# Layer 0's context quantisation: keys and values between the two turnings of the block maxima, and the fourth context's maxima one step sooner

## The chip, the cores and the metric

The kernel runs on one core of one Trainium2 chip. The metric is the device time of one execution in microseconds (us); lower is better. Engines are named as in the profile: PE is TensorE's matmul (PEld its weight loads), DVE VectorE, ACT ScalarE, POOL GpSimd, SP SyncE, which issues most DMAs.

## What is computed

A two-layer block on `x` (4 batches of 512 rows of 512) with a context `ctx_2048` (4 x 512 x 512). Cut to what matters:

```python
x = x + tanh(g_xattn[0]) * L0_xattn(layernorm(x), ctx_2048)
x = x + tanh(g_ffn[0])   * L0_ffn(layernorm(x), w1, w2)
x = x + tanh(g_xattn[1]) * L1_xattn(layernorm(x), ctx_2048, ctx_2048, ...)
x = x + tanh(g_ffn[1])   * L1_ffn(layernorm(x), ...)        # experts and a shared part
...
def L0_xattn(x, weight):                  # weight is the context
    xq = quant_dequant_act_1x128(x)       # FP8 rounding, one scale per row and 128 columns
    wq = quant_dequant_weight_128x128(weight)   # one scale per 128x128 block: its largest magnitude
    return einsum('emk,enk->emn', xq, wq)
...
K = (key @ Wk);  V = (value @ Wv)         # in L1_xattn, from the context as it was given
```

Layer 0 needs the context rounded block by block; layer 1's keys K and values V need it unrounded. `L0_ffn` has two products with weights rounded to -1, 0 and 1, rows rounded to 8 bits ahead of each, and two gelus between.

## The kernel before

**Row tiles and steps.** The 2048 rows are 16 tiles of 128 rows; tile t belongs to batch and context b = t // 4. `x_sb` holds all rows in SBUF. Layer 0 is a software pipeline written out by hand: `step(s, between)` runs for s = -7 to 15 and puts pieces of several tiles next to one another. For step s: the LayerNorm, the row maxima and the FP8 rounding of tile s+7 (`cross_rows`), the hidden scales of tile s-1 (`hidden_scales`, with the 128x2048 reduce `ham`), the first FFN product and two gelus of tile s (`hidden`), the cross product of tile s+6 (`cross_product`), then whatever is given as `between`, the second FFN product of tile s-2 (`down`), and the 8-bit rounding of rows for later tiles. From the written order a scheduler makes the final order of each engine's queue; ScalarE's gelus, squares and 8-bit roundings are pinned to the written order.

**A cross product** (`cross_product`): four turnings of the rounded rows `va` into PSUM (`tpa`, L754), a copy to SBUF on ScalarE (`vTa`, L758), four products with the rounded context (`oa`, L761; two passes each in float32), and the update of `x_sb` on VectorE (L768).

**A context** (`cross_context(b)`, L663 to L723) is a generator; each `yield` ends a piece and `go(ctx, n)` runs n pieces. The pieces before the change:
1. the block maxima along the rows of the transposed context (`cam`, L671; one 128x2048 reduce for b > 0), the first turning (`tpm`, L675), the largest of each block (`cpeak`, L677), spread over 128 columns (`cwide`, L679), the second turning (L680), and the scales `csafe` and `cup` (L682 to L686);
2. the keys: four matmuls of 512 columns (`k_ps`, L690) and a ScalarE copy (L697);
3. the values: 16 matmuls of 128 columns (`v_ps`, L702) and a ScalarE copy (L709);
4. to 7. for each quarter `dc`: the context times `cup` in place (L715, VectorE), four VectorE operations of FP8 rounding (`fp8_round`, L136 to L141), and four ScalarE multiplications by `csafe` (L722).

Keys and values read the context, and L715 overwrites it, so L715 waits for the last key and value product. Layer 0's cross product for tile 4b needs context b complete.

**Buffers.** `tpm`, `k_ps`, `v_ps`, `tpa`, `ob` and `tot_ps` share a PSUM pool of two buffers (`acc`); `oa` and `h_ps` share another of three (`big`). Contexts have three SBUF buffers. The transfer of context 3 (`load_batch(3)`) is written after step -3.

**Where pieces are placed.** Context 0 runs whole ahead of the steps. Contexts 1 and 2 are cut over steps -7 to -4 and -2 to 0, context 3 over steps 2 to 4:

```python
step(-7, [lambda: go(ctx1, 3)])
step(-5, [lambda: go(ctx1, 1)] + ...)
step(-4, [lambda: go(ctx1, 3), ...])
step(-2, [lambda: go(ctx2, 2)] + ...)
step(-1, [lambda: go(ctx2, 2)] + ...)
step(0, [lambda: go(ctx2, 3), ...])
step(1)
step(2, [lambda: go(ctx3, 3)])
step(3, [lambda: go(ctx3, 2)])
step(4, [lambda: go(ctx3, 2), ...])
```

**Reciprocal square roots** are powers on GpSimd: VectorE writes the variance (`ve_a`, `ve_b`) or the sum of squares (`nc_h`, `nc_x`), GpSimd raises it (`rstd_a`, `rstd_b`, `nc_*`), and VectorE goes on with the result (`va`, `vb` at L130; `ham` at L893). `layer_norm_stats` (L116 to L127) makes `ve_a` and `rstd_a` for the four tiles of a batch.

Of the kernel before, what the change touches and what calls it, by code (L numbers as in the profile page):

```python
# [20 lines left out]
P = 128  # L21
B, S, D = 4, 512, 512
NT = B * S // P
TB = S // P
DC = D // P
# [23 lines left out]
def flamingo_kernel(  # L49
# [22 lines left out]
    nc = tc.nc  # L72
# [9 lines left out]
    def acc(name):  # L82
        return ps_acc.tile([P, 512], F32, tag="acc", name=name)
# [26 lines left out]
    kT = kv[:, : B * S].rearrange("p (b s) -> p b s", b=B)  # L110
    v_sb = kv[:, B * S : 2 * B * S].rearrange("p (t n) -> p t n", n=NG * DH)
# [22 lines left out]
    def fp8_round(y, e):  # L134

        nc.vector.tensor_scalar(  # L136
            e.bitcast(I32), y.bitcast(I32), 0x7F800000, None, ALU.bitwise_and
        )
        nc.vector.tensor_scalar(e, e, 2.0**-6, 1.5 * 2.0**20, ALU.max, ALU.mult)
        nc.vector.tensor_tensor(y, y, e, ALU.add)  # L140
        nc.vector.tensor_tensor(y, y, e, ALU.subtract)  # L141
# [417 lines left out]
    with ExitStack() as l0:  # L559
# [9 lines left out]
        with ExitStack() as ph:  # L569
# [14 lines left out]
            def load_rows(b):  # L584
                for ts in [slice(t, t + 1) for t in range(TB)] if b == 0 else [slice(b * TB, b * TB + TB)]:
                    nc.sync.dma_start(out=x_sb[:, ts, :], in_=x_t[:, ts, :])
# [3 lines left out]
            wk_sb = wkv.tile([P, DC, NG * DH], F32, name="wk_sb")  # L590
            wv_sb = wkv.tile([P, DC, NG * DH], F32, name="wv_sb")
# [71 lines left out]
            def cross_context(b):  # L663


                c = state["ctx", b]
                cb = c.rearrange("p c (n q) -> p (c n) q", q=P)

                am = small.tile([P, 16], F32, tag="cam", name=f"cam_{b}", bufs=2)
                for ns in [slice(4 * dc, 4 * dc + 4) for dc in range(DC)] if b == 0 else [slice(16)]:  # L670
                    nc.vector.tensor_reduce(  # L671
                        am[:, ns], cb[:, ns, :], AX.X, ALU.max, apply_absolute_value=True
                    )
                tp = acc(f"tpm_{b}")
                nc.tensor.transpose(tp[:16, :P], am, ident)  # L675
                peak = small.tile([16, 1], F32, tag="cpeak", name=f"cpeak_{b}", bufs=2)
                nc.vector.tensor_reduce(peak, tp[:16, :P], AX.X, ALU.max)  # L677
                wide = small.tile([16, P], F32, tag="cwide", name=f"cwide_{b}", bufs=2)
                nc.vector.tensor_copy(wide, peak.to_broadcast([16, P]))  # L679
                nc.tensor.transpose(tp[:, P : P + 16], wide, ident[:16, :16])  # L680
                safe = small.tile([P, 16], F32, tag="csafe", name=f"csafe_{b}", bufs=2)
                nc.vector.tensor_scalar_max(safe, tp[:, P : P + 16], 1e-6)  # L682
                up = small.tile([P, 16], F32, tag="cup", name=f"cup_{b}", bufs=2)
                nc.vector.reciprocal(up, safe)
                nc.vector.tensor_scalar_mul(up, up, FP8_MAX)
                nc.vector.tensor_scalar_mul(safe, safe, 1.0 / FP8_MAX)  # L686
                yield
                k_ps = acc(f"k_ps_{b}")
                for dc in range(DC):
                    nc.tensor.matmul(  # L690
                        k_ps,
                        lhsT=wk_sb[:, dc, :],
                        rhs=c[:, dc, :],
                        start=dc == 0,
                        stop=dc == DC - 1,
                    )
                nc.scalar.copy(kT[:, b, :], k_ps)  # L697
                yield
                v_ps = acc(f"v_ps_{b}")
                for kc in range(TB):  # L700
                    for dc in range(DC):
                        nc.tensor.matmul(  # L702
                            v_ps[:, kc * P : (kc + 1) * P],
                            lhsT=c[:, dc, kc * P : (kc + 1) * P],
                            rhs=wv_sb[:, dc, :],
                            start=dc == 0,
                            stop=dc == DC - 1,
                        )
                nc.scalar.copy(  # L709
                    v_sb[:, b * TB : (b + 1) * TB, :], v_ps.rearrange("p (c n) -> p c n", c=TB)  # L710
                )
                yield
                for dc in range(DC):
                    ns = slice(dc * 4, dc * 4 + 4)
                    nc.vector.tensor_tensor(  # L715
                        cb[:, ns, :], cb[:, ns, :], up[:, ns].unsqueeze(2).to_broadcast([P, 4, P]),
                        ALU.mult,
                    )
                    e = apool.tile([P, 512], F32, tag="e", name=f"ce_{b}_{dc}")
                    fp8_round(c[:, dc, :], e)  # L720
                    for n in range(dc * 4, dc * 4 + 4):
                        nc.scalar.mul(cb[:, n, :], cb[:, n, :], safe[:, n : n + 1])  # L722
                    yield  # L723
# [200 lines left out]
            def at(t, *what):  # L924
                if 0 <= t < NT:
                    for f in what:
                        f(t)

            def go(pieces, n=1):
                for _ in range(n):  # L930
                    next(pieces, None)

            def step(s, between=()):

                rows = iter(())
                if s + 7 < NT:
                    rows = cross_rows(s + 7)
                at(s - 1, hidden_scales)
                go(rows)
                at(s, hidden)  # L940
                at(s + 6, cross_product)
                go(rows)
                for f in between:
                    f()
                at(s - 2, down)
                at(s - 1, hidden_quant)
                if s % TB == 0:
                    at(s + 4, row_stats)
                    at(s + 5, row_stats)
                elif s % TB == 1:  # L950
                    at(s + 5, row_stats)
                    at(s + 6, row_stats)
                    at(s + 3, row_norm)
                    at(s + 4, row_norm)
                elif s % TB == 2:
                    at(s + 4, row_norm)
                    at(s + 5, row_norm)
                at(s + 2, row_quant)
                at(s + 1, row_ready)

            with ExitStack() as first:
                stg = first.enter_context(tc.tile_pool(name="stg", bufs=4))
                ws = (w1T, w2T)
                wd = (w1q, w2q)
                load_batch(1)
                load_rows(1)
                load_weight(stg, 0, ws[0])
                load_batch(2)
                for b in range(2, B):
                    load_rows(b)  # L970
                go(cross_context(0), 7)
                cross_stats(0)

                def w(f, k, *cs):
                    return [lambda c=c: f(k, c, wd[k]) for c in cs]

                ctx1, ctx2 = cross_context(1), cross_context(2)
                step(-7, [lambda: go(ctx1, 3)])
                step(-6, w(weight_sum, 0, 0, 1))
                step(-5, [lambda: go(ctx1, 1)] + w(weight_sum, 0, 2, 3))  # L980
                weight_mean(0)
                scales_left(0)
                step(-4, [lambda: go(ctx1, 3), lambda: cross_stats(1)] + w(weight_round, 0, 0, 1))
                load_weight(stg, 1, ws[1])
                step(-3, w(weight_round, 0, 2, 3) + w(weight_sum, 1, 0))
                load_batch(3)
                step(-2, [lambda: go(ctx2, 2)] + w(weight_sum, 1, 1, 2, 3))
                weight_mean(1)
                scales_left(1)
                step(-1, [lambda: go(ctx2, 2)] + w(weight_round, 1, 0, 1, 2, 3))  # L990
            hpool = ph.enter_context(tc.tile_pool(name="hpool", bufs=2))
            state["hpool"] = hpool
            step(0, [lambda: go(ctx2, 3), lambda: cross_stats(2)])
            ctx3 = cross_context(3)
            step(1)
            step(2, [lambda: go(ctx3, 3)])
            step(3, [lambda: go(ctx3, 2)])
            step(4, [lambda: go(ctx3, 2), lambda: cross_stats(3)])
# [327 lines left out]
    for n in range(2):  # L1326
        m, f = rt(f"m{n}", 1), rt(f"f{n}", 1)
# [17 lines left out]
    for k in range(NT):  # L1345
        nc.tensor.matmul(
            pos[:, k * E :],
            lhsT=before if k == 0 else ones_h,
            rhs=flat[:, : (NT - k) * E],
            start=k == 0,  # L1350
            stop=k == NT - 1,
        )
    for t in range(NT):
        nc.tensor.matmul(
            pos_ps[:, 1, :E],
            lhsT=ones_h,
            rhs=taken[:, t, :],
            start=t == 0,
            stop=t == NT - 1,
# [38 lines left out]
    go = []  # L1398
    for n in range(2):
        w = rt(f"w{n}")  # L1400
# [235 lines left out]
```

## Time and profile before

| | us |
|---|---|
| median of three runs | 1257.39 (1257.39 to 1257.48) |
| the profiled execution | 1256.45 |
| its span (first to last instruction) | 1254.8 |
| outside the span | 1.65 |
| mean granted TensorE clock | 0.977 of full |
| layer 0's steps with context work | about 30 to 173 of the span |

How to read the views. Times count from the start of the span. A row of the busy-time table is one stretch: its borders, its length, then for PE, PEld, DVE, ACT and POOL the busy time with the number of instructions, the granted TensorE clock (1.00 is full), the mean busy share of the DMA engines and GB/s. A row of a waits list is the engine, what waited, what released it, and then the total time, how many times, and the longest. A timeline row is start, duration, engine, line, operation, output<-inputs, shapes and how many alike in a row; in brackets stands the idle time of the engine just ahead and what ended it. A float32 matmul of 128x512 appears as two passes, so four of them are x8.

The clock row of the page, in 40 equal slices of 31.4 us (9 is 90% or more of full), shows that the granted clock is mostly full:

```profile
PEclk9887999899999999999999999999999999999998
```

And the row for VectorE in the same slices; layer 0 is the first five or six:

```profile
DVE  7999999787457666656654511331221111111110
```

### The profile page before, as it was taken

The numbers are of one execution on the slowest core, as the hardware profiler recorded it, in microseconds if no ns is written. First come the engines' busy times: TensorE is split into PE (matmuls) and PEld (weight loads), VectorE is DVE, ScalarE is ACT, GpSimd is POOL, SyncE is SP. The second block draws the span as 40 slices with busy tenths as digits, with TensorE's granted clock in tenths as the row PEclk, the third lists the DMA queues.
The fourth block names the chain that finished last, engine by engine and source line by source line (L and its number), as shares of the span: only waits on it lengthen the run. The fifth ranks groups of instructions, "written<-read, shape, count | busy, mean of one in ns | idle before, by whom it ended". The sixth has DMA issues, their size and how long they took to land. (4 is left out here: it accounts for less than half of the span.)

```text
span 1254.8 us, 14322 instructions
## 1 busy us (share of the span) xinstructions
PE 1163.9 (93%) x5262; PEld 531.2 (42%) x5262; DVE 606.4 (48%) x1157; ACT 510.8 (41%) x710; POOL 412.7 (33%) x409
## 2 busy tenths in 40 slices
PE   5776988899899999999999999999999999999996
PEld 2432443343333333333333444444345555555553
DVE  7999999787457666656654511331221111111110
ACT  4889798595355554544454211100001112121211
POOL 1010010111467877767787301055001111111111
PEclk9887999899999999999999999999999999999998
DMA  9411222445011211211003000056316786888782
GB/s 345 152 66 25 43 43 54 92 84 127 5 65 35 68 36 35 69 35 60 2 1 143 9 1 1 0 201 212 85 66 187 229 270 195 261 259 252 207 261 35
DMA packets 88753, 135.32 MB, mean 108 GB/s; under 512 B 52837, under 2 KB 54121, under 8 KB 84841
## 3 DMA queue, kind: packets, MB, share of 16 engines
q1 hardware_dynamic: 80936, 116.52, 29.3%
q0 software_dynamic: 7744, 17.86, 6.5%
q8 instruction: 42, 0.69, 0.2%
q14 instruction: 31, 0.25, 0.1%
HBM read 113.84 MB, written 32.32 MB: 116 GB/s over the span
## 5 line engine op out<-in xcount | busy, mean ns | idle before, releaser
L428 ACT ACTIVATE ex<-s,mbias,mk 128x1024 f32<-128x1024 f32 x128 | 147.3, 1201 | 140.6 <-PE s L239 140.6
L319 DVE TENSOR_REDUCE nmax<-s 128x2 f32<-128x1024 f32 x128 | 150.3, 1215 | 98.8 <-PE s L239 88.0
L1475 PE MATMUL gue<-w,xT 128*128 128x352 f32 x576 | 176.3, 459 | 0.0
L1516 POOL DMA_INDIRECT out_dram<-ye,row_i x36 | 55.5, 1542 | 317.7 <-ACT ye L1515 219.5
L389 POOL TENSOR_TENSOR part<-part,ex 128x1024 f32<-128x1024 f32 x62 | 144.7, 2353 | 16.3 <-PE sm L239 11.4
L1219 PE MATMUL gu<-xnT_d,w 128*128 128x512 f32 x320 | 140.4, 593 | 0.7 <-ACT xnT_d L1173 0.7
L1475 PEld LDWEIGHTS gue<-w,xT 128*128 128x128 f32 x576 | 109.1, 190 | 70.4 <-issue 16.9
L1498 DVE COPY hT<-tph_e 128x256 f32<-128x256 f32 x36 | 15.3, 425 | 248.6 <-PE tph_e L1495 248.6
L1506 PE MATMUL oe<-w,hT 128*128 128x512 f32 (+1 forms) x216 | 102.3, 609 | 3.2 <-DVE hT L1498 0.5
L1219 PEld LDWEIGHTS gu<-xnT_d,w 128*128 128x128 f32 x320 | 59.9, 190 | 73.9 <-issue 72.1
L1207 ACT ACTIVATE sg<-gu,sgb 128x512 f32<-128x512 f32 x20 | 13.7, 687 | 176.8 <-PE gu L1219 176.8
L761 PE MATMUL oa<-ctx,vTa 128*128 128x512 f32 x128 | 65.9, 662 | 19.1 <-ACT vTa L758 19.1
L389 POOL TENSOR_TENSOR part<-ex,ex 128x1024 f32<-128x1024 f32 x32 | 75.8, 2391 | 23.0 <-ACT ex L428 23.0
L1484 ACT ACTIVATE sge<-gue 128x352 f32<-128x352 f32 x35 | 16.3, 466 | 147.3 <-PE gue L1475 147.3
L239 PE MATMUL s<-row_tables 10*128 10x512 bf16 (+1 forms) x512 | 67.7, 384 | 9.2 <-DVE nmax L319 5.7
L239 PE MATMUL s<-k,qT 32*128 32x512 f32 x512 | 72.4, 605 | 0.4 <-ACT qT L287 0.4
L239 PE MATMUL s<-qT,k 32*128 32x512 f32 x512 | 71.6, 598 | 0.0
L912 PE MATMUL ob<-w2q,hqT 128*128 128x512 bf16 x256 | 62.2, 396 | 9.4 <-DVE hqT L838 9.4
L239 PE MATMUL av<-ex,kv 128*32 128x512 f32 x512 | 69.2, 605 | 0.4 <-ACT ex L428 0.4
L1208 DVE SCALAR_TENSOR_TENSOR hd<-gu,sub,sg 128x512 f32<-128x512 f32 x20 | 15.0, 750 | 111.5 <-ACT sg L1207 111.5
L239 PE MATMUL q_ps<-xnT,wq_sb 128*128 128x512 f32 (+1 forms) x156 | 68.6, 552 | 0.0
L239 PE MATMUL oc<-wo,attnT 128*128 128x512 f32 (+1 forms) x164 | 66.2, 525 | 0.0
(262 smaller groups left out, 1649.7 us busy)
## 6 DMA issues: line engine op xcount, KB each, us to landing
w<-in_e_w_dram SPq DMA_DIRECT2D x36, 1408.0 KB
w<-in_e_w_dram SPq DMA_DIRECT2D x36, 768.0 KB
slots<-row_tables SPq DMA_DIRECT2D x13, 771.0 KB
xr<-slots SPq DMA_DIRECT2D x36, 256.0 KB
stage<-in_w1T_dram SPq DMA_DIRECT2D x4, 1024.0 KB
stage<-in_w2T_dram SPq DMA_DIRECT2D x4, 1024.0 KB
k<-kv SPq DMA_DIRECT2D x64, 64.0 KB
out_dram<-x_sb SPq DMA_DIRECT2D x16, 256.0 KB
```

Source lines behind the costliest of these rows:

```text
L239: tc.keep_in_program_order(nc.tensor.matmul(*args, **how))
L319: largest = nc.vector.tensor_reduce(nmax[:, i, 2 * j : 2 * j + 2], sc[j], AX.X, ALU.max, negate=True)
L389: nc.gpsimd.tensor_tensor(part[:, hs, :], old[:, hs, :], ex[:, hs, :], ALU.add)
L428: nc.scalar.activation(ex[:, 2 * j : 2 * j + 2, :], sc[j], AF.Exp, bias=mbias[:, b, kc : kc + 1], scale=mk[:, b, kc : kc + 1],)
L761: nc.tensor.matmul(o_ps[:, 0, :], lhsT=vT[:, dc, :], rhs=cq[:, dc, :], start=dc == 0, stop=dc == DC - 1,)
L912: nc.tensor.matmul(o_ps, lhsT=hqT[:, c, :], rhs=w2q[:, c * D : (c + 1) * D], start=c == 0, stop=c == IC - 1,)
L1219: nc.tensor.matmul(gu[:, m, :], lhsT=w[:, dc, c * P : (c + 1) * P], rhs=xnT[:, dc, b * S : (b + 1) * S], start=dc == 0, stop=dc == DC - 1,)
L1475: nc.tensor.matmul(gu[:, m, :I], lhsT=xT[:, dc, :], rhs=wt[:, dc, :], start=dc == 0, stop=dc == DC - 1,)
L1484: nc.scalar.activation(sg, gu[:, 0, :I], AF.Silu)
L1498: nc.vector.tensor_copy(hT[:, :2, :], tp[:, : 2 * P].rearrange("p (c q) -> p c q", q=P))
L1506: nc.tensor.matmul(o_ps[:, 0, :], lhsT=hT[:ni, c, :], rhs=dw[:ni, c, :], start=c == 0, stop=c == len(ICH) - 1,)
L1516: added = nc.gpsimd.indirect_dma_start(out=out, out_offset=bass.IndirectOffsetOnAxis(ap=row_i[:, j, 0:1].bitcast(I32), axis=0), in_=y, in_ ...
```

## The change

Keys and values become an inner generator `keys_values`. For contexts 1 to 3 it now runs after `cwide` and ahead of the second turning, with one more `yield` before it; the second turning, `csafe` and `cup` follow after the values. Context 0 keeps its order. The placement follows the new count of pieces: four instead of three of context 1 in step -7, three instead of two of context 2 in step -1; and context 3's first piece (maxima, first turning, `cpeak`, `cwide`) is given to step 1, its next three to step 2.

```diff
@@ cross_context
+                def keys_values():
+                    k_ps = acc(f"k_ps_{b}")
...
+                    nc.scalar.copy(kT[:, b, :], k_ps)
+                    yield
+                    v_ps = acc(f"v_ps_{b}")
...
+                    yield
...
                 nc.vector.tensor_copy(wide, peak.to_broadcast([16, P]))
+                if b > 0:
+                    yield
+                    yield from keys_values()
                 nc.tensor.transpose(tp[:, P : P + 16], wide, ident[:16, :16])
                 safe = small.tile([P, 16], F32, tag="csafe", name=f"csafe_{b}", bufs=2)
                 nc.vector.tensor_scalar_max(safe, tp[:, P : P + 16], 1e-6)
...
                 nc.vector.tensor_scalar_mul(safe, safe, 1.0 / FP8_MAX)
                 yield
-                k_ps = acc(f"k_ps_{b}")
...
-                yield
-                v_ps = acc(f"v_ps_{b}")
...
-                yield
+                if b == 0:
+                    yield from keys_values()
                 for dc in range(DC):
...
-                step(-7, [lambda: go(ctx1, 3)])
+                step(-7, [lambda: go(ctx1, 4)])
...
-                step(-1, [lambda: go(ctx2, 2)] + w(weight_round, 1, 0, 1, 2, 3))
+                step(-1, [lambda: go(ctx2, 3)] + w(weight_round, 1, 0, 1, 2, 3))
...
-            step(1)
+            step(1, [lambda: go(ctx3)])
             step(2, [lambda: go(ctx3, 3)])
```

The matmuls and copies inside `keys_values` are those that stood there before, unchanged.

More of the change, by code (lines that the diff above doesn't have):

```diff
@@ L667, in cross_context @@
                 cb = c.rearrange("p c (n q) -> p (c n) q", q=P)
+                def keys_values():
+                    k_ps = acc(f"k_ps_{b}")
+                    for dc in range(DC):
+                        nc.tensor.matmul(
+                            k_ps,
+                            lhsT=wk_sb[:, dc, :],
+                            rhs=c[:, dc, :],
+                            start=dc == 0,
+                            stop=dc == DC - 1,
+                        )
+                    nc.scalar.copy(kT[:, b, :], k_ps)
+                    yield
+                    v_ps = acc(f"v_ps_{b}")
+                    for kc in range(TB):
+                        for dc in range(DC):
+                            nc.tensor.matmul(
+                                v_ps[:, kc * P : (kc + 1) * P],
+                                lhsT=c[:, dc, kc * P : (kc + 1) * P],
+                                rhs=wv_sb[:, dc, :],
+                                start=dc == 0,
+                                stop=dc == DC - 1,
+                            )
+                    nc.scalar.copy(
+                        v_sb[:, b * TB : (b + 1) * TB, :], v_ps.rearrange("p (c n) -> p c n", c=TB)
+                    )
+                    yield
                 am = small.tile([P, 16], F32, tag="cam", name=f"cam_{b}", bufs=2)
@@ L687, in cross_context @@
                 yield
-                k_ps = acc(f"k_ps_{b}")
[L689 to L697, printed above, removed]
-                yield
-                v_ps = acc(f"v_ps_{b}")
[L700 to L711, printed above, removed]
-                yield
+                if b == 0:
+                    yield from keys_values()
                 for dc in range(DC):
```

## Prediction, written before the changed kernel ran

> **What bounds the kernel now.** I read the page first, then busy time by stage, then the waits of TensorE and VectorE in the stage that the edit touches, then the timelines around the fourth context.
>
> ```profile
> PE 1163.9 (93%) x5262; PEld 531.2 (42%) x5262; DVE 606.4 (48%) x1157; ACT 510.8 (41%) x710; POOL 412.7 (33%) x409
> ```
>
> Over the whole span TensorE looks like the bound. That is an average. All moved instructions lie in layer 0, and in the built instruction order of the changed kernel every queue is back in the old order at the reduce `ham_5` (L888, 172.98 us on VectorE). So the stage is 29.8 to 173 us, here with the two after it:
>
> ```profile
> core 0: us, PE busy (x) PEld busy (x) DVE busy (x) ACT busy (x) POOL busy (x), PEclk, DMA share, GB/s
> 29.80:173.00 143.20, 110.30 (x404) 56.86 (x405) 136.83 (x379) 123.96 (x222) 11.99 (x12) 0.87 0.26 72
> 173.00:213.00 40.00, 32.12 (x129) 14.39 (x128) 37.38 (x106) 33.55 (x49) 3.87 (x5) 1.00 0.26 50
> 320.00:790.00 470.00, 459.67 (x2740) 170.77 (x2735) 247.51 (x267) 199.42 (x224) 285.98 (x272) 1.00 0.11 38
> ```
>
> VectorE is busy 136.83 of 143.20 us (96%), TensorE 110.30 (77%). The roles turn only later (459.67 of 470 for TensorE). VectorE leads this stage and has 6.4 us of idle time in it. The waits say whose:
>
> ```profile
> PE oa L761 <- ACT vTa L758: 15.8, 8, 7.0
> PE tpm L680 <- DVE cwide L679: 7.7, 2, 5.5
> PE k_ps L690 <- DVE csafe L682: 1.1, 1, 1.1
> ```
> ```profile
> DVE ham L893 <- POOL nc_h L788: 2.1, 4, 0.7
> DVE vb L130 <- POOL rstd_b L804: 1.8, 2, 0.9
> DVE x_sb L768 <- PE oa L761: 1.7, 3, 0.8
> ```
>
> The first list (us, times, longest) has what the edit aims at: TensorE stands at the second turning for 7.7 us. The second shows that little of it reaches VectorE, which waits for a TensorE result only 1.7 us in all. The large wait, in TensorE's queue:
>
> ```profile
> 117.16 0.33 PE L754 MATMUL tpa<-ident,va 128*128 128x128 f32 x1
> 123.00 0.28 PE L680 MATMUL tpm<-ident,cwide 16*128 16x16 f32 x1 [5.51 <-DVE cwide L679]
> 124.35 2.08 PE L690 MATMUL k_ps<-ctx,wk_sb 128*128 128x512 f32 x2 [1.07 <-DVE csafe L682]
> 126.22 4.51 PE L761 MATMUL oa<-ctx,vTa 128*128 128x512 f32 x8
> 133.14 3.73 PE L702 MATMUL v_ps<-wv_sb,ctx 128*128 128x128 f32 x32
> ```
>
> **The change part by part.** The instruction set is the same on every engine: no work is added or removed, and VectorE's 136.83 us stay. cross_context issues no DMA, SP's queue is unchanged, and POOL's only swaps one hidden-scale power with the power for `rstd_a`. Only VectorE's idle time can change, so I laid its new order out with the durations of before and took the difference of each wait.
>
> *Context 1* (three more pieces at step -7): TensorE does all 16 value products before the second turning instead of 5, turning, 11. With `v_ps_1` unsplit, `oa_0` and `oa_1` come about 0.7 us sooner, and two VectorE waits of 0.32 and 0.09 go: -0.41.
>
> *Context 2*: keys go ahead of the turning, whose first wait (7.7 - 5.5 = 2.2 us on TensorE) is filled. Values are split 6 and 10 around `oa_5`, not 8 and 8. The scaling L715 rewrites `ctx` and must wait for the last value product; VectorE now comes there earlier, and gives back +0.36. The scheduler also moves `ve_a_8` (85.35 us before) to directly ahead of `va_8`: 0.74 us of work lie between, where the same power round trip shows 1.31 to 1.73 us elsewhere in the trace (start to start). I take 1.4: +0.65 (bounds +0.57 and +0.99). Queued behind it are the LayerNorm rows of tile 8, then ACT's `va_8` scalings.
>
> *Context 3* (maxima at step 1, keys and values at step 2). The block reduce `cam_3` (2.28 us at 108.71) goes 2.6 us earlier. It then stands ahead of the x-updates L768 of `oa_6` and `oa_7`, whose waits were 0.60 and 0.76; about 0.1 of the first is left: -1.26. On TensorE the first turning goes behind `oa_7`, the second into `tpa_8`; the waits of 5.51 and 1.07 go. All four key products (3.6 us) run at about 117.7 to 121.3, in that gap. Then TensorE has nothing: `oa_8` waits for `vTa_8`, which on ACT stands behind `va_9`'s scalings (4 in 1.28 us) and the first gelu of `h_2` (2.09), and those scalings wait for `xup_9`, which VectorE now makes at 121.3, not 112.3. 121.3 + 1.28 + 2.09 + 0.5 = 125.1: a new wait of 3.8 us in place of 6.6.
>
> Here a rule bears on the sum. The rows first:
>
> ```profile
> 53.00:56.40 3.40, 1.12 (x3) 0.65 (x4) 3.40 (x9) 3.40 (x7) 0.75 (x1) 1.00 0.62 196
> 56.40:59.80 3.40, 3.40 (x6) 1.32 (x5) 3.40 (x10) 3.40 (x6) 0.64 (x1) 0.50 0.94 308
> ```
>
> A 4.00-us wait ended at 55.27 in a stretch with 1.12 us of TensorE work, yet the next 3.4 us were granted half the clock, and the eight `oa` passes took 5.40 us, not the 3.70 of a full-rate row. The Trainium skill ("TensorE: Matmul & The Clock Gate", section "What's actually happening") says that the clock halves after at least one idle window of about 3.4 us and returns after one busy window. By that rule, with the windows' phase left open, a gap of 3.8 us holds a whole idle window rarely ((3.8 - 3.4)/3.4, 12%), `oa_8` runs at full rate, and `v_ps_3` ends at 125.1 + 3.7 + 3.5 = 132.3, before VectorE needs `ctx`: no stall. By the row the clock halves until about 128.0 (the stretches lie on a 3.4-us grid, at 121.2, 124.6, 128.0): 2.9 us do 1.45 us of work, the other 2.25 end at 130.25, and values at 133.8. I take the row, as it is a measurement of such a gap.
>
> VectorE comes to `ctx_3` x `cup` (L715) at 132.8. Before it came at 136.69 and found the values just done:
>
> ```profile
> 136.37 0.41 DVE L139 TENSOR_SCALAR xe<-xe 128x512 f32<-128x512 f32 x1
> 136.69 0.68 DVE L715 TENSOR_TENSOR ctx<-ctx,cup 128x512 f32<-128x512 f32 x1
> ```
>
> Now it waits 133.8 - 132.8 = +1.0 (bounds 0 by the rule, 4.2 below). Behind the waiting instruction stand `xup_11`, the statistics of the fourth context, the `ob_0` update and `ham_2`; ACT's `va_11` scalings and `hq_2` wait for those, but ACT has slack (123.96 of 143.2 busy). Small ones: the first `vb_4` waits 1.08, not 0.91 (+0.17); `ham_0` +0.1, `oa_8` +0.1, `ham_3` +0.2; several waits under 0.1 go, -0.25. `ob_0` is 2.8 us earlier on TensorE; its reader on VectorE comes later anyway, so that is worth nothing.
>
> Sum: -0.41 + 0.36 + 0.65 - 1.26 + 1.0 + 0.17 + 0.1 + 0.1 + 0.2 - 0.25 = +0.66 us at 173 us. From there the order is identical and VectorE still leads (37.38 of 40), so the shift is carried to the end. The profiled execution took 1256.45 us (span 1254.8 and 1.65 outside it), so 1257.1; the median of the runs is 0.94 above that execution: 1257.39 + 0.66, about 1258.0 us.
>
> **The rivals.** 0.2% (2.5 us) is about what a measurement of this kernel can tell from no change; the chances count against that bound.
>
> *A, as summed*: VectorE leads, TensorE's gain is slack, +0.66 with single terms off by a microsecond or two: 1256 to 1259.8. Chance 0.58. That the change does not do what it says (scheduler restores the old order) is excluded by the built order; a net of nothing from cancelling waits lies in this case, another 0.04.
>
> *B, faster: the TensorE-ACT chain is the real leader.* VectorE's 96% would then be partly elastic, its rows following what TensorE releases. TensorE loses 5.51 + 1.07 + 2.2 = 8.8 us of waits and gets 3.8 back: 5.0 us, 1252.4. For it: TensorE's wait total (34 us) and the late `v_ps_3` that ends within 0.2 us of where VectorE needs it. Against: VectorE's waits for it are 1.7 us, so more than that can't come from this stage by the trace. A part of it (the clock staying full: -1.0; two POOL round trips covered: -1) remains within 0.2%. Later half-rate stretches (237, 312, 326 us) may also fall differently, 1.7 us each in a full TensorE. Chance 0.18.
>
> *C, slower: the new gap costs the clock for longer.* After the 7-us wait of before, half clock lasted from 93.9 to 104.2, through the whole `oa` (6.54 us):
>
> ```profile
> 98.40 6.54 PE L761 MATMUL oa<-ctx,vTa 128*128 128x512 f32 x8 [7.03 <-ACT vTa L758]
> ```
>
> If the 3.8-us gap does likewise (half rate to 134.8), `oa_8` ends at 131.7, values at about 137.0, and VectorE stands 4.2 us at `ctx_3` instead of 1.0: 0.66 + 3.2 = +3.9, 1261.3. It decides as soon as the values end after 135.6, where the stall passes 2.8 us and the sum 2.5. A `vTa_8` that is 2 us later on ACT has the same end. For it: VectorE comes to `ctx_3` 3.9 us sooner than before, while TensorE ends the values only 3.1 us sooner. Against: the gap is half as long and the grid reopens at 128.0. Chance 0.20.
>
> **How the numbers follow.** A and the cancelling case: same, 0.62; B faster, 0.18; C slower, 0.20. The likeliest's own range is 1256 to 1259.8. For 8 in 10, the range goes over C's value (1261.5) and to the near part of B (1253.6, a gain of 3.8), which leaves out about half of B and the tail of C.
>
> **What would show it.** Right: TensorE's waits at L680 and L690 nearly gone, a wait of 3 to 4 us for `vTa` at `oa_8`; granted clock 0.5 somewhere in 124 to 128; VectorE's list with a new `ctx` L715 on TensorE `v_ps` of about 1.0 (and 0.4 for context 2), a new `va` L130 on POOL of 0.65, and `x_sb` on `oa` down from 1.7 to some 0.3; `ham_5` starting within 1 us of 172.98, and all later marks shifted alike. Wrong: `ham_5` over 2.5 us away from 172.98 (B if early, C if late with a long L715 wait), or an unchanged `ham_5` with a different end, which would put the difference in stages that the edit does not touch.

## The result, and the profile after

The changed kernel takes 1261.64 us (median of eight, 1259.67 to 1263.58) against 1257.39 (median of eight runs of before beside them): 1.0034 times the time before, 95% interval 1.0025 to 1.0043. It is slower by about 4.2 us. The profiled execution is the longest of the eight: 1263.58, span 1261.8.

First the place. I paired each VectorE row of the new trace with its row in the old one. "Lag" below is the new start less the old one, both counted from the same early row (the third L136 of context 0, 26.05 us before), so that a different start of the first loads drops out.

| VectorE row | start before | lag after |
|---|---|---|
| x-update of tile 3 (context 1 is done) | 61.63 | +0.93 |
| x-update of tile 7 | 113.25 | +0.37 |
| x-update of tile 8 | 130.77 | +2.06 |
| `ham_5`, where the orders join again | 172.98 | +2.26 |
| x-update of tile 11 | 175.18 | +4.09 |
| `ham_15`, the last such reduce of layer 0 | 293.31 | +4.13 |

(So layer 0 reaches to about 300 us, the tenth slice of the rows above; the first five or six slices hold its context work.) Between tile 7 and `ham_5` VectorE's rows stand in another order, so there a lag is partly a changed place. In sum about 0.9 us arise at context 1, 1.3 more by `ham_5`, and 1.8 in the one step after `ham_5`, where the queues are already the old ones. The 4.13 of this one execution are close to the 4.2 between the medians. What comes after 300 us differs between the profiles (last section).

The busy time of the same stretch, and the waits of TensorE there (the same window as before):

```profile
29.80:173.00 143.20, 106.19 (x383) 52.92 (x387) 134.84 (x371) 121.99 (x220) 11.13 (x12) 0.89 0.25 70
```
```profile
PE oa L769 <- ACT vTa L766: 20.8, 10, 6.1
...
PE tpa L762 <- DVE csafe L713: 3.6, 1, 3.6
PE ob L920 <- DVE hqT L846: 3.1, 1, 3.1
```

(Lines in the changed file stand some eight lower: L761 is L769, L768 is L776, L902 is L910.) The 7.7 us at the second turning are gone. In their place stand 5.0 us more at the cross products, a new 3.6 at tile 0's turning and 3.1 instead of 1.5 at a down product; the 1.1 us ahead of context 3's keys are still there. VectorE's busy time in the window fell by 2.0 us: it got less far. Its longest waits from 57 us to `ham_5`:

```profile
DVE x_sb L776 <- PE oa L769: 2.2, 2, 1.4
DVE vb L130 <- POOL rstd_b L812: 1.9, 2, 1.0
DVE ham L901 <- POOL nc_h L796: 1.3, 3, 0.4
DVE va L130 <- POOL rstd_a L126: 0.5, 1, 0.5
DVE ctx L723 <- PE v_ps L684: 0.4, 1, 0.4
```

Now the three places. **Context 1**, TensorE, before and then after:

```profile
31.15 4.97 PE L702 MATMUL v_ps<-wv_sb,ctx 128*128 128x128 f32 x22
...
37.28 3.70 PE L761 MATMUL oa<-ctx,vTa 128*128 128x512 f32 x8 [0.73 <-ACT vTa L758]
```
```profile
35.12 0.63 PE L762 MATMUL tpa<-ident,va 128*128 128x128 f32 x4 [3.60 <-DVE csafe L713]
36.88 5.23 PE L769 MATMUL oa<-ctx,vTa 128*128 128x512 f32 x8 [1.13 <-ACT vTa L766]
```

Before, the wait for `cwide` (2.2 us) lay ahead of the value products. These ran at half clock (22 passes in 4.97 us), which held the cross product up by a few tenths at most, and the clock was full again for the cross product. After, the values run early and at full rate, the gap lies directly ahead of tile 0's turning and cross product, and it is that product, which VectorE needs, that runs in part at half clock (0.70 granted over its length): it begins 0.40 us sooner and ends 1.13 us later.

**Context 3** is the same picture, larger:

```profile
119.15 3.70 PE L672 MATMUL k_ps<-ctx,wk_sb 128*128 128x512 f32 x8 [1.06 <-DVE csafe L713]
126.48 6.51 PE L769 MATMUL oa<-ctx,vTa 128*128 128x512 f32 x8 [3.63 <-ACT vTa L766]
```

Keys at full rate, a gap of 3.63 us, then `oa_8` at a granted clock of 0.56 over its whole length. Before, the gaps of 5.51 and 1.07 us were there too, but the first part of the half clock fell on two key passes (2.08 us); `oa_8` took 4.51. How much of the product falls into the half clock is not fixed by the queue: in the second profile of the changed kernel (below), behind the same gap, it took less:

```profile
126.83 5.40 PE L769 MATMUL oa<-ctx,vTa 128*128 128x512 f32 x8 [3.63 <-ACT vTa L766]
```

**The tail.** ScalarE's queue before, then after: context 3's last scalings (L722, now L730) and behind them, pinned, the 8-bit rounding of tile 3's hidden rows (L902, now L910):

```profile
159.42 2.46 ACT L722 ACTIVATE ctx<-ctx,csafe 128x128 f32<-128x128 f32 x8
161.75 2.02 ACT L902 ACTIVATE hq<-h,hqs 128x2048 int16<-128x2048 f32 x1
```
```profile
163.88 1.28 ACT L730 ACTIVATE ctx<-ctx,csafe 128x128 f32<-128x128 f32 x4 [1.49 <-DVE ctx L141]
165.06 1.99 ACT L910 ACTIVATE hq<-h,hqs 128x2048 int16<-128x2048 f32 x1
```

In the new order VectorE rounds the last quarter later (its last L141 starts at 163.16, before at 156.63), ScalarE waits for it with the rounding queued behind, and the rounded rows reach VectorE (`hqT`, L846) and TensorE later. TensorE's queue, before and then after:

```profile
169.44 2.12 PE L912 MATMUL ob<-w2q,hqT 128*128 128x512 bf16 x9 [1.49 <-DVE hqT L838]
171.40 3.60 PE L761 MATMUL oa<-ctx,vTa 128*128 128x512 f32 x8
```
```profile
172.19 3.15 PE L920 MATMUL ob<-w2q,hqT 128*128 128x512 bf16 x9 [3.10 <-DVE hqT L846]
175.13 4.30 PE L769 MATMUL oa<-ctx,vTa 128*128 128x512 f32 x8
```

The down product of tile 3 waits 3.1 us for its turned rows (1.49 before), the cross product of tile 11 stands behind it, and VectorE waits at the x-update of tile 11, where it did not wait before. The granted clock just behind the gap, and that wait:

```profile
173.00:175.80 2.80, 2.80 (x8) 1.23 (x6) 2.77 (x9) 2.60 (x5) 0.00 (x0) 0.52 0.02 6
```
```profile
179.47 0.75 DVE L776 SCALAR_TENSOR_TENSOR x_sb<-oa,tg,x_sb 128x512 f32<-128x512 f32 x1 [1.76 <-PE oa L769]
```

So the clock is in the tail too. The down product starts with a lag of 2.55 us, only 0.3 more than VectorE's at `ham_5`. But from its start to the end of the cross product it is 7.24 us (172.19 to 179.43), and before it was 5.56 (169.44 to 175.00). These 1.68 us are nearly the whole 1.83; before, behind the gap of 1.49 us, the clock stayed full.

### The profile page after: what moved, and what is told of

Same layout as the page of the kernel before. It is cut to its first block, busy times and chain, and to the rows that moved or that the text cites. A ratio compares the mean times of both kernels' runs of the same rounds, so it can differ in the third digit from the quotient of the medians.

```text
span 1261.8 us, 14312 instructions
## 1 busy us (share of the span) xinstructions
PE 1167.4 (93%) x5246; PEld 530.9 (42%) x5262; DVE 606.8 (48%) x1157; ACT 511.3 (41%) x710; POOL 411.6 (33%) x409
## 5 line engine op out<-in xcount | busy, mean ns | idle before, releaser
L769 PE MATMUL oa<-ctx,vTa 128*128 128x512 f32 x128 | 70.0, 697 | 23.8 <-ACT vTa L766 23.8
```

The source lines that it names most:

```text
L769: nc.tensor.matmul(o_ps[:, 0, :], lhsT=vT[:, dc, :], rhs=cq[:, dc, :], start=dc == 0, stop=dc == DC - 1,)
```

## The experiments

All ratios are to the kernel before on the same chip. Three groups ran together: the four kernels from "context 1 alone" to "contexts 2 and 3" (before: 1256.69), the four from "context 1's turnings" to "keys twice" (before: 1263.44), and "changed, again" with the last three rows (before: 1265.34). In the last two groups before is 7 to 9 us slower than in the first, and the traces have 7 to 8 us more between 800 and 900 us, so between groups only lags and ratios are compared.

"Lag" is that of the one profiled execution, always against the same profile of before. It is not exact: in the last row the edit acts from 160 us on, and yet the lag is +0.30 at tile 3 and +0.54 at tile 7. And the profiled execution need not be a typical one: with context 3 alone it is 5 us longer than the median, with four scalings late and context 1 back it is the fastest of its seven.

| kernel | ratio, 95% interval | lag at tile 3 | at `ham_5` | at tile 11 | at `ham_15` |
|---|---|---|---|---|---|
| changed | 1.0034 (1.0025 to 1.0043) | +0.93 | +2.26 | +4.09 | +4.13 |
| changed, again | 1.0040 (1.0027 to 1.0054) | +2.41 | +1.69 | +3.52 | +3.47 |
| context 1 alone | 1.0014 (1.0005 to 1.0023) | +1.03 | +0.80 | +0.80 | +0.76 |
| context 2 alone | 1.0043 (1.0030 to 1.0056) | +0.41 | +1.38 | +3.37 | +4.25 |
| context 3 alone | 1.0054 (1.0038 to 1.0070) | +0.42 | +3.39 | +6.76 | +8.08 |
| contexts 2 and 3 | 1.0022 (1.0013 to 1.0031) | -0.31 | +1.12 | +2.95 | +2.94 |
| context 1's turnings in the other pool | 1.0039 (1.0027 to 1.0051) | +0.79 | +0.08 | +1.91 | +3.33 |
| last two quarters late | 1.0050 (1.0037 to 1.0063) | +2.57 | +4.37 | +4.87 | +6.83 |
| both of these | 1.0047 (1.0034 to 1.0060) | +0.68 | +1.54 | +2.05 | +4.07 |
| context 3's keys twice | 1.0070 (1.0057 to 1.0083) | +0.89 | +3.55 | +6.29 | +7.44 |
| four scalings late | 1.0049 (1.0035 to 1.0063) | +2.02 | +0.51 | +0.51 | +4.92 |
| four scalings late, context 1 back | 1.0031 (1.0020 to 1.0042) | -0.11 | -1.54 | -1.54 | -0.02 |
| before, four scalings late | 0.9990 (0.9981 to 0.9999) | +0.30 | +0.60 | +0.60 | +0.72 |

### The parts alone

Theory: stalls at separate places that add up. Context 1 alone:

```diff
-                if b > 0:
+                if b in (1,):
                     yield
                     yield from keys_values()
...
-                if b == 0:
+                if b not in (1,):
                     yield from keys_values()
...
-                step(-1, [lambda: go(ctx2, 3)] + ...)
+                step(-1, [lambda: go(ctx2, 2)] + ...)
...
-            step(1, [lambda: go(ctx3)])
+            step(1)
```

> Only context 1 has its keys and values ahead of the second turning; contexts 2 and 3 as in the kernel before. Against before, only 24 rows of VectorE's queue and the place of one TensorE turning differ. Theory (stalls at separate places that add up; here the first turning of tile 0 waits for the scale csafe of context 1, because both use one of the two small PSUM buffers): a TensorE wait of 3.6 us for csafe near 35 us, the first cross product at half clock (5.2 us), VectorE 1.0 us late from 56 us on, and +1.0 us at the end. Rival (only the end of context 3's work sets the time, and a delay of 1 us at 56 us is absorbed by later waits): within 0.3 us of before.

Measured 1.0014, +1.6 us between the medians; lag +1.03 at tile 3 and +0.76 at the end of layer 0. In this queue the delay of context 1 is carried, not absorbed.

Context 2 alone and context 3 alone (the same edit with `(2,)` or `(3,)`, with their steps):

> Only context 2 has its keys and values ahead of the second turning. In the built order this alone moves xup of tile 9 behind the hidden reduce of tile 1 on VectorE, puts ScalarE's scalings of tile 9 ahead of the gelu of tile 2, and moves the rounding of context 3's last quarter next to the hidden reduce of tile 4, as in the changed kernel. Theory: the loss between 100 and 190 us comes from those two moved places, whoever moves them: +2.5 to +3.4 us. Rival (the loss comes from the fourth context's maxima standing a step sooner): within 0.5 us of before.

> Only context 3 is changed, with its maxima a step sooner. Its queues are row for row those of a kernel that has the maxima a step sooner and keeps the old order of keys and turning. Theory: the same two moved places as in the kernel with context 2 alone, so +2.5 to +3.4 us, with a wait of 3 to 4 us at the cross product of tile 8, half clock there, and a wait of about 3 us of the down product of tile 3 for its turned rows. Rival (each of the contexts 2 and 3 costs a part of its own): about +1.5.

Measured 1.0043 and 1.0054. Each alone costs as much as the whole change or more, and more than theory and rival had. That each of them costs a share of its own, which sum up, falls: together they cost 1.0022. Context 2 alone has maxima that stand no step sooner, and yet `hq` of tile 3 is late (TensorE waits 6.64 us for `hqT` at 173), so the sooner step is not the cause by itself. For context 3 the order of keys and turning in the text changes no row of any queue: with the sooner step alone the built order is the same (noted above before the run). My reading is that what costs is where the scheduler puts the rows of tile 9 and of context 3's last quarter once something ahead of them has moved; no run holds these two places fixed.

Contexts 2 and 3 (the changed kernel with context 1 put back):

> The changed kernel with context 1 put back (keys and values after the scales, three pieces in step -7). Theory of adding stalls: the changed kernel less 1.0 us, so +3.2 us against before. Rival (context 1's delay is absorbed by later waits): +4.2 as the changed kernel.

Measured 1.0022, +2.4 us (lag +2.94). At all four marks its lag is 1.1 to 1.2 us under that of the changed kernel (against the second profile of the changed kernel: 2.7 at tile 3, but 0.5 at `ham_15`). So about 1 us of context 1 and some 3 of the other two add.

### Context 1: a buffer, or a gap?

The turning of tile 0 waited for `csafe`, since `tpm` and `tpa` share a pool of two buffers. This edit gives context 1's turnings a large buffer instead:

```diff
-                tp = acc(f"tpm_{b}")
+                tp = big(f"tpm_{b}")[:, 0, :] if b == 1 else acc(f"tpm_{b}")
```

> The changed kernel, with the turnings of context 1 in the other PSUM pool (three large buffers), so that tile 0's turning doesn't have to wait for the scale csafe of context 1. TensorE's queue is row for row that of the changed kernel; on VectorE csafe, cup and 8 rows around change places. Theory (buffer): the 3.6-us wait is gone, the first cross product runs at full clock, and the time is that of the changed kernel less 1.0 to 1.2: +3.1 against before. Rival (context 1 is late because its scales come later on VectorE, whoever holds the buffer): no gain, +4.2.

The lag at tile 3 is +0.79, hardly less than +0.93. My theory fell. The wait for `csafe` is gone, and others fill the same gap:

```profile
32.05 0.28 PE L711 MATMUL tpm<-ident,cwide 16*128 16x16 f32 x1 [3.30 <-DVE cwide L707]
33.96 1.36 PE L762 MATMUL tpa<-ident,va 128*128 128x128 f32 x4 [1.62 <-ACT va L755]
37.20 5.70 PE L769 MATMUL oa<-ctx,vTa 128*128 128x512 f32 x8 [1.88 <-ACT vTa L766]
```

TensorE has run out of work ahead of the cross product, whoever it waits for, and the product runs at half clock. What this costs is shown by the changed kernel's second profile, where the half-clock stretch fell differently on the same product in the same queue:

```profile
36.70 6.62 PE L769 MATMUL oa<-ctx,vTa 128*128 128x512 f32 x8 [1.13 <-ACT vTa L766]
```

It took 6.62 us instead of 5.23, 1.39 more, and the lag at tile 3 was 2.41 instead of 0.93, 1.48 more. At tile 3 this time has gone to VectorE one for one. It did not last, though: by `ham_5` the second profile lags less than the first (1.69 against 2.26). VectorE, later, no longer waits 0.80 us at the x-update of tile 7, and at tile 8 it waits 0.25 and not 1.36, since `oa_8` took 5.40 us and not 6.51. So where the half clock falls shifts the parts of one kernel's sum by 1 us and more, while the whole stays about the same (+4.13 and +3.47).

> The changed kernel once more, unaltered, beside the next three on one chip, so that they can be compared with it there. All theories: +4.2 us against before (1.0034).

Measured 1.0040 (1.0027 to 1.0054) on the slower chip, which agrees with 1.0034. The kernel with the other pool, 1.0039, is no better than this.

### Context 3: the half clock

```diff
-                    for dc in range(DC):
+                    for dc in [*range(DC)] * (2 if b == 3 else 1):
                         nc.tensor.matmul(k_ps, ...)
```

The keys of context 3 are computed twice, with one result.

> The changed kernel, with the four key products of context 3 issued twice (the second set starts the sum anew, so the keys are the same): about 3.7 us more TensorE work in the gap ahead of the cross product of tile 8. The scheduler also changes the place of some VectorE rows of context 3 with it. Theory: the clock stays full, the cross product takes 3.7 us and not 6.5, VectorE's 1.36-us wait at the update of tile 8 goes; but VectorE regains that wait by 149 us anyway and the later waits set the end, so the time is within 1 us of the changed kernel. Rival (the halved clock is the cause of the loss): 2.5 to 2.8 us less than the changed kernel.

```profile
119.71 7.13 PE L672 MATMUL k_ps<-ctx,wk_sb 128*128 128x512 f32 x16 [1.06 <-DVE csafe L713]
127.04 3.70 PE L769 MATMUL oa<-ctx,vTa 128*128 128x512 f32 x8 [0.20 <-ACT vTa L766]
```

With the gap filled the product takes 3.70 us, not 6.51 or 5.40, and from tile 7 to tile 8 VectorE loses 0.24 us instead of 1.69 or 0.57 (the two profiles of the changed kernel). Locally the clock is the cause. The total got worse, though, 1.0070: the scheduler changed other rows with it, `hq` of tile 3 came later still, and its down product waited 7.82 us. So this run proves the local price, and says nothing on the end.

### The tail

The last two quarters of context 3 written behind tile 3's rounding:

```diff
-            step(4, [lambda: go(ctx3, 2), lambda: cross_stats(3)])
+            step(4, [lambda: cross_stats(3)], [lambda: go(ctx3, 2)])
```

(`step` runs the new last argument behind `hidden_quant`.)

> The changed kernel, with the last two quarters of context 3 written behind the 8-bit rounding of tile 3's hidden rows in step 4, so that ScalarE rounds those rows first. Theory (the late last quarter holds back the rounding hq of tile 3, its transfer, the down product of tile 3, and the cross product of tile 11 behind it on TensorE): hq of tile 3 about 3.5 us sooner than in the changed kernel, TensorE's 3.1-us wait for hqT gone or under 1.5, no VectorE wait at the update of tile 11, and 1.5 to 2.2 us less than the changed kernel: about +2.3 against before. Rival (VectorE is late already, or the wait moves on to tile 4's hidden rows): within 0.5 us of the changed kernel, +4.

Measured 1.0050: no gain. The wait moved, as the rival had it, though not to tile 4: the scheduler now put an earlier quarter late, the rounding of tile 2 stood behind that one, and tile 2's down product waited 4.45 us for `hqT` (at 160.42).

Both repairs together:

> The changed kernel with both repairs, the other PSUM pool for context 1's turnings and context 3's last two quarters behind the rounding of tile 3's hidden rows. Theory of adding stalls: 2.5 to 3.2 us less than the changed kernel, +1.3 against before; what is left is the cross product of tile 8 at half clock and the new VectorE waits near 120 to 136 us. Rival (one bound behind both): no more than the better of the two repairs.

Measured 1.0047: neither repair brings a gain, so their sum brings none.

A finer edit moves only ScalarE's four scalings of the last quarter, and leaves VectorE's rows in place up to about 168 us:

```diff
-                    for n in range(dc * 4, dc * 4 + 4):
-                        nc.scalar.mul(cb[:, n, :], cb[:, n, :], safe[:, n : n + 1])
+                    def give_back(dc=dc):
+                        for n in range(dc * 4, dc * 4 + 4):
+                            nc.scalar.mul(cb[:, n, :], cb[:, n, :], safe[:, n : n + 1])
+                    if b == 3 and dc == 3:
+                        state.setdefault("back", []).append(give_back)
+                    else:
+                        give_back()
...
+            step(4, [lambda: go(ctx3, 2), lambda: cross_stats(3)], [lambda: [f() for f in state.pop("back")]])
```

> The changed kernel, but only ScalarE's four scalings of context 3's last quarter are written behind the rounding of tile 3's hidden rows; VectorE's work on that quarter stays where it is (its queue is the same up to row 400, about 168 us). Theory (in ScalarE's queue these scalings wait 1.5 us for VectorE and hold back hq of tile 3, and so its transfer, the down product of tile 3, and the cross product of tile 11): hq of tile 3 starts 2.5 to 3.5 us sooner, TensorE's 3.1-us wait for hqT falls under 1, VectorE's 1.8-us wait at tile 11's update goes, and the time is 1.5 to 2 us less than the changed kernel: about +2.4 against before. Rival (the half clock in front of tile 8 has made everything late and the tail only follows): within 0.5 us of the changed kernel.

ScalarE and TensorE then:

```profile
160.36 1.99 ACT L916 ACTIVATE hq<-h,hqs 128x2048 int16<-128x2048 f32 x1
162.25 1.26 ACT L731 ACTIVATE ctx<-ctx,csafe 128x128 f32<-128x128 f32 x4
```
```profile
167.46 2.33 PE L926 MATMUL ob<-w2q,hqT 128*128 128x512 bf16 x10 [0.31 <-DVE hqT L852]
```

The rounding starts at 160.36 instead of 165.06, the 3.1-us wait is 0.31, the clock stays full there (`oa_11` takes 3.70 us), and the jump from `ham_5` to tile 11 is gone (+0.51 and +0.51; +2.26 and +4.09 in the changed kernel, +1.69 and +3.52 in its second profile). So the jump comes of the late rounding, by the gap that it leaves ahead of the down product and the half clock behind it; with the earlier rounding the scheduler also put VectorE's conversion of these rows (`hqT`) further forward. The gain was not kept: behind row 400 VectorE's order differs, the row maxima of tiles 13 and 14 come later, a cross product waits 2.80 us for `vTa` at 202 us and runs 5.23 us, at half clock again, and by `ham_15` the lag is +4.92 (1.0049 in all).

The same on contexts 2 and 3:

> The same edit on the kernel with context 1 put back. Theory of adding stalls: both recoveries, 2.5 to 3 us less than the changed kernel, +1.3 against before, what is left being the waits between 100 and 173 us. Rival: no more than the 1.0 to 1.4 us that putting context 1 back gives, +3.

Here layer 0 ends level with before (lag -0.02, after -1.54 at tile 11). The ratio is still 1.0031 (1.0020 to 1.0042). Its profiled run, the fastest of the seven and 2.3 us under their median, loses 1.6 us more near 330 us (last section); what the other runs lose, and where, is open.

And on the kernel before:

> The kernel before, with the same edit of ScalarE's queue alone (four scalings behind one rounding). There TensorE waits 1.5 us for tile 3's turned hidden rows, but VectorE does not wait at tile 11's update. Theory (VectorE leads; only a stall that reaches it counts): within 0.4 us of before. Rival (TensorE's wait counts by itself): 1 to 1.5 us faster than before.

VectorE's lag does not fall (+0.63 at tile 8, ahead of the edit's place, and +0.60 at tile 11), as the theory has it. The time does not agree: the ratio, 0.9990 (0.9981 to 0.9999), is a gain of 1.3 us, which is what the rival forecast and more than the theory allowed. No row of the profile shows where it comes from, and the interval only just leaves out 1, so that VectorE's lag alone sets the time is not settled by this run. No other run beats either kernel.

## Why the prediction was wrong

It gave 1258.0 in 1253.6 to 1261.5, with "same" likeliest. Measured: 1261.64. The sum that it put at +0.66 us came as about +4.1 in the profiled run: 1.34 of the difference at context 1, 1.83 behind `ham_5`, 0.3 between. What failed in both large places is that the half clock was charged to one product alone, `oa_8`. Point by point:

- **What leads** held in the main. VectorE's waits account for the lag of the profiled run, and TensorE's 7.7 us at the turning bought nothing.
- **Context 1, -0.41: wrong in sign, +0.93.** The step that failed is "`oa_0` and `oa_1` come about 0.7 us sooner": I moved the value products forward and did not ask what TensorE does in the time set free. It stood 3.60 us ahead of tile 0's turning, which with the clock (5.23 for 3.70) made a gain of 0.40 at the start of the product into a loss of 1.13 at its end. That the turning waits for `csafe` through a shared buffer was not in my sum either; taking that buffer away showed that it is not what decides.
- **Context 2, +0.36 and +0.65**: the first did not come as a wait; the second came as 0.5. Small. The 2.2-us wait that I put here was context 1's (30.93 us); context 2's second turning had no wait before.
- **Context 3.** The gap was right (3.8 forecast, 3.63 measured), and the row that I took over the rule as well: the clock did halve after a gap of under 4 us. In this profile the half clock lasted longer than I had it: I had full rate from 128.0, and `oa_8` in 5.15 us; it ran at 0.56 on the mean, 6.51. In the second profile it took 5.40, near the forecast, so this term depends on where the half clock falls. The single terms did not hold: 1.36 us at the x-update of tile 8 where I had 0.1, 0.40 at L715 (now L723) where I had 1.0, and of the 1.26 us to be won at tiles 6 and 7 only 0.56, as tile 7 still waits 0.80. That the sum from context 1 to `ham_5` is +1.3 (2.26 less 0.93), near the +1.07 of my terms without context 1, is luck.
- **From `ham_5` on, "the order is identical ... so the shift is carried to the end": wrong by 1.83 us.** An identical order carries a shift only if everything that it meets is equally late. Ahead of tile 3's down product, TensorE's own last turning was 0.9 us late, and VectorE's `hqT`, which the product waits for, 2.5. So the gap of 1.49 us, which stands in the trace of before, became 3.10, and the half clock behind it cost 1.68 us. I had charged no clock there. `hq` of tile 3 started 3.3 us later on ScalarE (165.06 against 161.75); I had written that "ACT has slack (123.96 of 143.2 busy)", but an engine's mean load says nothing of one pinned instruction behind a late one.
- **Rival C** had the figure (+3.9) and half of its mechanism, the half clock through most of `oa_8`. Its price did not come where it said (4.2 us at `ctx`; measured 0.40), and what made up the rest was context 1 and the tail, which it did not name. That its figure fits is luck.

What the runs leave open: why contexts 2 and 3 cost more alone than together. The traces name the tail there too (waits of 6.64 and 5.38 us for `hqT`), but what the scheduler weighs in placing the last quarter was not tested. Open too is the whole time: each place was mended in some run, but none of the changed kernels came back to the time of before, not even the one whose profile ends layer 0 level with it.

## What to carry to other kernels

Filling a wait of TensorE moves the wait; look at which product then stands directly behind each gap, old gaps that grow included, and reckon there with half clock. In these profiles, from 25 to 345 us, a gap of 3 us and more was followed by half clock with one exception (3.36 us at 211 us, four scalings late with context 1 back); a gap of some 2 us sometimes was. How much of the product it takes differs from one execution to the next (5.23 and 6.62 us for the same one), so read such a term from more than one profile. Where a scheduler orders the queues, an edit at one place is an edit of all queues behind it: follow each pinned instruction of an in-order engine to what stands ahead of it, and take the waits that the old trace already shows there as gaps that can grow. Two queues that agree from some row on do not mean that the engines arrive together.

## What I had not expected of the hardware

In the changed kernel's profiled run, about 1.3 us are lost near 330 us, and 1.4 more near 630, in layer 1, where no instruction differs. At the first place the cause shows in the clock (before, then after; the rows cover the first products after a gap of some 2 us):

```profile
328.00:332.00 4.00, 4.00 (x28) 1.57 (x24) 2.35 (x2) 0.42 (x1) 0.00 (x0) 0.82 0.01 4
```
```profile
332.00:336.00 4.00, 4.00 (x16) 1.70 (x16) 2.35 (x2) 0.00 (x0) 0.00 (x0) 0.50 0.00 0
```

The half-clock stretch begins at another point of the same work, and TensorE, busy for the whole of both rows, does 16 passes instead of 28 in 4 us. Of the profiles here seven lose 1.3 to 1.6 us at this place: the changed kernel (twice), context 3 alone, the keys twice, four scalings late (with and without context 1 put back), and context 1's turnings in the other pool. Two of them (the other pool, and four scalings late on the whole change) had gained 1.7 us just ahead, at about 315 us, where before has half clock and they have not. That is likely a good part of why one kernel's runs differ by up to 4 us (1259.67 to 1263.58); that it is, was not measured run by run. Near 630 us it is alike: the changed kernel's granted clock is 0.50 from 630.5 to 633.9 us, where before has no half clock, and the changed kernel (twice), context 3 alone, the keys twice and four scalings late lose 1.4 to 1.5 us there.
